# Product 6 of the down parts, and product 5 of the conditioner's, as seven quarter products; scales loaded one number at a time

## The chip, the core and the metric

The kernel runs on one core of a Trainium2 chip. TensorE (PE) multiplies, with its weight loads shown apart as PEld; VectorE (DVE), ScalarE (ACT) and GpSimd (POOL) do the elementwise work; SyncE (SP), ACT and POOL issue the DMAs. The metric is the device time of one execution in microseconds (us). Lower is better. A line number such as L627 is a line of the kernel before.

## The reference

There are 1024 tokens of 512 features in x (8 sequences of 128). Two layers follow each other, each a "conditioner" and a feed-forward part, and each adds its result to x:

```
x = x + L0_ffn(L0_cond(x))
x = x + L1_ffn(L1_cond(x))

L0_cond:  act  = silu(x Wg' + low-rank) * (x Wu' + low-rank)      F = 1376
          down = act Wd' + low-rank(act)                          512 features
L0_ffn:   w_eff = w * (su @ sv)   (for gate, up and down)         I = 1792
          down = (silu(h gate') * (h up')) down'
L1_cond:  x W' + b + 2 * low-rank(x)                              512 x 512
L1_ffn:   W[o, i] = q[o, i] * s[o, i // 128]   (q are small integers)
          down = (silu(h Wg') * (h Wu')) Wd'                      I = 1792
```

The scales of the last part are s_gu, one number for each of 1792 rows, 2 matrices and 4 groups of features, and s_down, one for each of 512 rows and 14 groups. On the chip they are wanted as sg, 128 partitions by 112 numbers, and sd, 128 partitions by 56 numbers.

## The kernel before, in words

Features lie on the partitions (x and h are each four tiles of 128 x 1024) and the tokens along the row, in two halves of 512 (tb = 0 and 1). The stages, by their times in the profile: the conditioner's gate and up (tiles p_c, until 157 us), the conditioner's down part (d_c, 157 to 231), the feed-forward gate and up (p_f, 231 to 397), its down part (d_f, 397 to 481), the last conditioner (l, 481 to 512) and the quantised feed-forward part (gu_q and d_q, to the end).

Both down parts are the one function down() (L601). It is given n blocks of 128 inner features: n = 11 in the conditioner (layer "c", 5 pairs and one left over), n = 14 in the feed-forward part (layer "f", 7 pairs). The output of 512 features by 1024 tokens, seen as a 2 x 2 matrix of blocks, is made by Winograd's seven products in place of eight. Each product has two output tiles m of 128 x 512. The weight forms of the products are a[1] to a[7], and the token forms are called 11, 12, 21, 22 and T1 to T4: T1 = 12 - 11 for product 5, T3 = 22 - 12 for product 7, T2 = 22 - T1 for product 6, T4 = 21 - T2 for product 4. VectorE makes T1 to T4, by one subtraction for each pair (form, L630), and they overwrite dead forms.

A product is carried out in one of two ways. sums() does it whole: a matmul of 128 x 512 for each pair and each m. of_blocks() (L689) applies the same scheme once more inside it: one pair is done plainly, and the other 2 x group pairs (group is 2 in c, 3 in f) as seven quarter products of 128 x 256. In exchange these need token forms of their own (second_tokens, L649: four subtractions on VectorE, 512 columns wide in c, 768 in f), weight forms (second_weights, L661: four operations on POOL), two more PSUM banks z1 and z5, three copies on ACT into a tile r (L718, L722, L725), one addition on VectorE (odd, L627), and the additions of r onto the result. Before the change products 2, 3, 7 and 4 are done of blocks, and 1, 5 and 6 whole. "u" is product 1 plus product 6 and "v" the sum made from product 7; both are added onto several output tiles by VectorE.

The order on each engine is that of the program text (in_order pins it), so an instruction that waits holds up everything behind it on its engine. VectorE's order through the second half of down() is: the tokens of product 3, T3, additions for product 2, tokens of product 7, additions for product 3, T2, T4, tokens of product 4, additions of v, of u, of product 4. In c a hook (three_forms, hook 6) then makes forms T1, T3 and T2 of h for p_f, and T4 is made after the part. In f the last conditioner begins with l_T, the forms of x, T3 first.

There are eight PSUM banks, taken in turn, and r has two buffers. The weight forms s2 also have two. In f, POOL has behind its down work the gathers for the last conditioner's adapters, l_forms (four operations) and the DMAs of the quantised weights wgu_q and wd_q.

The scales are loaded by SP as rows (g_rows 112 x 128 and d_rows, 14 rows), turned by TensorE against an identity matrix, and copied from PSUM to SBUF by VectorE (turn_scales, hook 3, L1298 to L1304), in the middle of the d_f part. The identity is made on POOL.

The ACT engine makes, in each unit of p_c, a Silu that PE's banks wait for; in units f = 2 to 6 it also casts a piece of the feed-forward layer's scales (L453), which SP loads by 12 DMAs a piece (scale_raw, L445). The DMAs of SP and ACT share eight semaphores in turn, and each issue waits for the DMA that was given the same semaphore eight issues earlier.

Of the kernel before, what the change touches and what calls it, by code (L numbers as in the profile page):

```python
# [55 lines left out]
def kernel(  # L56
# [30 lines left out]
    def mm(*args, **kwargs):  # L87
        in_order(nc_mm(*args, **kwargs))  # L88
# [331 lines left out]
    for i, bit in enumerate((2 * RS, RS)):  # L420
# [3 lines left out]
        for low in range(2):  # L424
# [3 lines left out]
            )  # L428

    def scale_piece(pool, i: int):  # L430

# [168 lines left out]

    def down(pool, layer: str, n: int, act, wd0: int, to, plus: bool, dt, hooks, adapters=None):  # L601

# [38 lines left out]


        groups = [slice(i * group, (i + 1) * group) for i in range(2)]
        tokens2 = pool.tile([P, 4, group, quarter], F32, tag="tokens2", name=f"tokens2_{layer}")
        own = [tokens2[:, i] for i in range(4)]
        dead = [b["11"][:, g, bass.ts(q, quarter)] for g in groups for q in range(2)]
        second = {}

        def second_tokens(i: int, src: str, place, in_place: bool):  # L649

            b11, b12, b21, b22 = (
                b[src][:, g, bass.ts(q, quarter)] for g in groups for q in range(2)
            )
            t1, t2, t4, t3 = place
            if in_place:
                t3 = b12
            for t, x1, x2 in ((t1, b12, b11), (t2, b22, t1), (t4, b21, t2), (t3, b22, b12)):
                subtracted(t, x1, x2)
            second["b", i] = {1: b11, 2: b21, 3: b22, 4: t4, 5: t1, 6: t2, 7: t3}

        def second_weights(i: int):  # L661
            a11, a12, a21, a22 = (a[i][:, g, bass.ts(m, P)] for m in range(2) for g in groups)
            s = pool.tile([P, 3, group, P], F32, tag="s2", name=f"s2_{layer}{i}", bufs=2)
            s1, s2, s4 = (s[:, k] for k in range(3))
            weight_forms(nc.gpsimd, a11, a12, a21, a22, s1, s2, s4, True)
            second["a", i] = {1: a11, 2: a12, 3: s4, 4: a22, 5: s1, 6: s2, 7: a21}
# [26 lines left out]
        def of_blocks(i: int, src: str, onto=None, single=None):  # L693
# [4 lines left out]
            for m in range(2):  # L698
                mm(
                    banks[m], a[i][:, pairs - 1, bass.ts(m, P)], b[src][:, pairs - 1],  # L700
                    start=onto is None, stop=True, skip_group_check=onto is not None,
                )
                if single is not None and n % 2:
                    leftover(banks[m], m, *single)
            r = pool.tile([P, 4, quarter], F32, tag="r", name=f"r_{layer}{i}", bufs=2)

# [25 lines left out]

        def onto_output(i: int, src: str, banks, tb: int, more=lambda m: None):
            banks, r = of_blocks(i, src, banks, (0, tb))
            for m in range(2):
                more(m)
                if plus:
                    added(nc.vector, at(m, tb), banks[m], at(m, tb))
                else:
                    in_order(nc.scalar.copy(at(m, tb), banks[m]))  # L740
            for m in range(2):
                added(nc.gpsimd, at(m, tb), at(m, tb), r[m])
# [3 lines left out]
        for j in range(pairs):  # L746
            added(nc.vector, a[5][:, j], wd[1][0][:, j], wd[1][1][:, j])
            form_of(j, "T1", "12", "11")
        second_tokens(2, "21", own, False)
        subtracted(a[6], a[5], a[1])  # L750
        subtracted(a[3], a[2], a[6])
        second_weights(2)
        subtracted(a[7], a[1], a[7])
        banks1, banks5, banks4 = [], [], None
        for m in range(2):
            banks1.append(sums(1, m, "11"))
            in_order(nc.scalar.copy(u[m], banks1[m]))
        hook(1)
        for m in range(2):
            banks5.append(sums(5, m, "T1"))  # L760
        second_tokens(3, "22", dead, False)
        second_weights(3)
        form("T3", "22", "12")
        if adapters is None:
            for m in range(2):
                added(nc.vector, at(m + 2, 1), banks5[m], at(m + 2, 1))
            onto_output(2, "21", banks1, 0)
        else:
            def first_adapters(m: int):
                extra = new(8, m)  # L770
                leftover(extra, m, 1, 1, True)
                adapters(m, [[banks1[m], None], [None, extra]], go_on={(0, 0), (1, 1)})
                in_order(nc.scalar.copy(at(m + 2, 1), extra))
                added(nc.vector, at(m + 2, 1), banks5[m], at(m + 2, 1))

            onto_output(2, "21", banks1, 0, first_adapters)
        second_tokens(7, "T3", own, True)
        second_weights(7)
        if adapters is None:
            onto_output(3, "22", banks5, 1)  # L780
        else:
            banks4 = [new(4, m) for m in range(2)]

            def second_adapters(m: int):
                adapters(
                    m, [[None, banks5[m]], [banks4[m], None]], fresh={(1, 0)}, go_on={(0, 1)},
                )

            onto_output(3, "22", banks5, 1, second_adapters)
        second_weights(4)  # L790
        hook(2)
        form("T2", "22", "T1")
        form("T4", "21", "T2")
        second_tokens(4, "T4", dead, True)
        hook(3)
        banks7, v = of_blocks(7, "T3")
        for m in range(2):
            added(nc.vector, v[m], banks7[m], v[m])
            for tb in range(NTB) if plus else (1,):
                added(nc.vector, at(m + 2, tb), at(m + 2, tb), v[m])  # L800
        for m in range(2):
            added(nc.vector, u[m], sums(6, m, "T2"), u[m])
            for o in (m, m + 2):
                added(nc.vector, at(o, 1), at(o, 1), u[m])
            added(nc.vector, at(m + 2, 0), at(m + 2, 0) if plus else v[m], u[m])
        hook(6)
        banks4, r = of_blocks(4, "T4", banks4, (1, 0))
# [6 lines left out]
    with ExitStack() as c_layer:  # L814
# [116 lines left out]
        for f in range(NF0):  # L931
# [12 lines left out]
            if 3 <= f < 7:  # L944
                down_adapters_a.gather(range(2 * f - 6, 2 * f - 4))
            if f == 8:
                down_adapters_a.arrange(nc.scalar.copy, slice(0, NB))
# [42 lines left out]
        with ExitStack() as top:  # L990

            dt = [x[j // 2][:, bass.ts(j % 2, TB)] for j in range(NF0 // 2)]
            down(
                pool(top, "down_c", "right"), "c", NF0, act_c, NF - NF0, h, False, dt,
                {1: down_low_rank, 6: three_forms}, down_adapters,
            )

# [279 lines left out]

    one = early.tile([P, P], F32, tag="one", name="one")  # L1280
    in_order(nc.gpsimd.memset(one, 1.0))
    for sign in (1, -1):
        in_order(
            nc.gpsimd.affine_select(
                out=one, in_=one, pattern=[[-sign, P]], compare_op=ALU.is_ge,
                fill=0.0, base=0, channel_multiplier=sign,
            )
        )
    g_rows = early.tile([NF * 2 * KC, P], F32, tag="g_rows", name="g_rows")
    nc.sync.dma_start(out=g_rows, in_=s_gu.rearrange("f (c p) -> (f c) p", p=P))  # L1290
    d_rows = early.tile([NF, KC, P], F32, tag="d_rows", name="d_rows")
    nc.sync.dma_start(out=d_rows, in_=s_down.rearrange("f (k p) -> f k p", p=P))
    sg = early.tile([P, NF, 2, KC], F32, tag="sg", name="sg")
    sd = early.tile([P, KC, NF], F32, tag="sd", name="sd")

    def turn_scales():
        ps = bank("scales")
        n = NF * 2 * KC  # L1298
        mm(ps[:, :n], g_rows, one[:n, :n], start=True, stop=True)
        nc.vector.tensor_copy(sg.rearrange("p f s k -> p (f s k)"), ps[:, :n])  # L1300
        ps = bank("scales_down")
        for o in range(KC):
            mm(ps[:, bass.ts(o, NF)], d_rows[:, o, :], one[:NF, :NF], start=True, stop=True)
        nc.vector.tensor_copy(sd.rearrange("p o f -> p (o f)"), ps[:, : KC * NF])  # L1304

    lw = early.tile([P, KC, H], F32, tag="lw", name="lw")
# [16 lines left out]
    with ExitStack() as top:  # L1323
# [3 lines left out]
            down_f, "f", NF, act_all, 0, x, True, [dt[:, j] for j in range(NF // 2)],  # L1327
            {2: for_last_conditioner, 3: turn_scales},
        )
# [157 lines left out]
    def down_group(f: int, o: int, on_act=False):  # L1487
        w, src, scale = ready["q", f][1][:, bass.ts(o, P)], acts["q", f], sd[:, o, f : f + 1]
        both = pair(f"d_q{f}_{o}")
# [118 lines left out]
    def down_out(back: int, o: int, tb: int):  # L1608
        to = x[o][:, halves[tb]]
        f = last_f - back  # L1610
        scaled(to, groups["d", back, o, tb], sd[:, o, f : f + 1], to)
        store(o, tb)

    def down_copied(back: int, o: int, tb: int):
# [6 lines left out]
        f = last_f - back  # L1621
        scaled(ys[back, o, tb], groups["d", back, o, tb], sd[:, o, f : f + 1])

# [111 lines left out]
```

## Time and profile before

| | |
|---|---|
| times of 3 runs | 680.10, 678.46, 680.25 us, median 680.1 |
| the profiled execution | 678.08 us, span 676.4 us |
| granted TensorE clock | 0.997 |
| PE busy | 664.3 us (98%) |
| VectorE busy | 501.2 us (74%) |
| POOL busy | 408.8 us (60%) |
| ACT busy | 193.8 us (29%) |
| d_c, 157 to 231 us | PE 74.0 of 74, VectorE 56.4 |
| d_f, 397 to 481 us | PE 81.7 of 84, VectorE 78.1 |
| l, 481 to 512 us | PE 31.0 of 31, VectorE 19.1 |

The share over the whole span says that TensorE is nearly always busy. The table by stage says more: in d_f VectorE is nearly as full as TensorE. A row of the timeline gives the start, the duration, the engine, the line, the operation, the tiles (out<-in), the shape and how many instructions are drawn together; in brackets stands the idle time ahead of it and what ended that. A matmul of fp32 is recorded as two rows, so "x28" are 14 matmuls. Consecutive VectorE instructions overlap a little, so that a row of 0.67 us costs 0.60 us of the engine.

### The profile page before, as it was taken

The numbers are of one execution on the slowest core, as the hardware profiler recorded it, in microseconds if no ns is written. First come the engines' busy times: TensorE is split into PE (matmuls) and PEld (weight loads), VectorE is DVE, ScalarE is ACT, GpSimd is POOL, SyncE is SP. The second block draws the span as 40 slices with busy tenths as digits, with TensorE's granted clock in tenths as the row PEclk, the third lists the DMA queues.
The fourth block names the chain that finished last, engine by engine and source line by source line (L and its number), as shares of the span: only waits on it lengthen the run. The fifth ranks groups of instructions, "written<-read, shape, count | busy, mean of one in ns | idle before, by whom it ended". The sixth has DMA issues, their size and how long they took to land.

```text
span 676.4 us, 7209 instructions
## 1 busy us (share of the span) xinstructions
PE 664.3 (98%) x2520; PEld 405.1 (60%) x2520; DVE 501.2 (74%) x661; ACT 193.8 (29%) x292; POOL 408.8 (60%) x357
## 2 busy tenths in 40 slices
PE   8999999999999999999999999899999999999995
PEld 3444444444565645665666664685636777788874
DVE  6545435446749887878788679999747888899997
ACT  1212111211021112333323320110115655665563
POOL 5356765441344055667866931597702989898996
PEclk9999999999999999999999999999999999999998
DMA  6501125130002002202200060000851130000003
GB/s 237 197 1 53 63 78 183 63 140 1 0 1 78 31 0 94 93 13 82 94 0 1 0 208 0 1 0 17 292 175 30 41 86 16 16 1 1 1 1 124
DMA packets 18335, 42.48 MB, mean 63 GB/s; under 512 B 3118, under 2 KB 4286, under 8 KB 18172
## 3 DMA queue, kind: packets, MB, share of 16 engines
q1 hardware_dynamic: 11772, 25.71, 11.1%
q0 software_dynamic: 5376, 14.49, 6.9%
q10 hardware_dynamic: 1152, 1.84, 0.8%
q8 instruction: 20, 0.33, 0.2%
q14 instruction: 15, 0.12, 0.0%
HBM read 39.93 MB, written 2.10 MB: 62 GB/s over the span
## 4 chain that ended last, share of the span: by engine, by line
PE 84%; DVE 6%; POOL 6%; issue 2%; DMA 1%; ACT 1%; SPq 0%; POOLq 0%; DVEq 0%; ACTq 0%
PE p_c L88 21%; PE p_f L88 15%; PE gu_q L1450 12%; PE d_c L88 8%; PE d_q L1450 5%; PE d_f L88 4%; PE l L88 4%; PE zb_f L88 3%; PE za_f L88 3%; PE z_f L88 2%; PE z_c L88 2%; DVE act_f L630 1%; POOL sum L1465 1%; PE bank L1450 1%; POOL act_lo L1465 1%
## 5 line engine op out<-in xcount | busy, mean ns | idle before, releaser
L1459 DVE SCALAR_TENSOR_TENSOR sum<-gu_q,sg,sum 128x1024 f32<-128x1024 f32 x65 | 83.0, 1282 | 15.6 <-ACT sum L1456 10.3
L1450 PE MATMUL gu_q<-h_hi,wgu_q 128*128 128x512 f32 x208 | 82.2, 395 | 0.5 <-DVE l_v L1394 0.4
L1450 PE MATMUL gu_q<-h_lo,wgu_q 128*128 128x512 f32 x208 | 81.1, 390 | 0.0
L88 PE MATMUL p_f<-x,s_f 128*128 128x512 f32 x112 | 52.2, 597 | 0.0
L1456 ACT ACTIVATE sum<-gu_q,sg 128x1024 f32<-128x1024 f32 x39 | 43.3, 1113 | 21.9 <-PE gu_q L1450 21.8
L1465 POOL TENSOR_TENSOR sum<-sum,sum 128x1024 f32<-128x1024 f32 (+1 forms) x14 | 32.6, 2328 | 26.8 <-DVE sum L1459 26.8
L1450 PEld LDWEIGHTS gu_q<-h_hi,wgu_q 128*128 128x128 f32 x208 | 39.0, 188 | 13.0 <-DVE x L1459 2.5
L589 DVE TENSOR_TENSOR act_c<-p_c,v_c 128x512 f32<-128x512 f32 x11 | 7.6, 690 | 52.3 <-PE p_c L88 52.3
L1450 PEld LDWEIGHTS gu_q<-h_lo,wgu_q 128*128 128x128 f32 x208 | 39.1, 188 | 7.9
L88 PE MATMUL p_c<-x,raw_c 128*128 128x512 f32 x88 | 43.2, 616 | 0.0
L1465 POOL TENSOR_TENSOR act_lo<-sum,act_hi 128x1024 fp32r<-128x1024 f32 (+1 forms) x15 | 34.0, 2265 | 13.3 <-ACT act_hi L1517 13.3
L1459 DVE SCALAR_TENSOR_TENSOR x<-d_q,sd,x 128x1024 f32<-128x1024 f32 x33 | 42.0, 1275 | 0.0
L88 PE MATMUL p_c<-T_x,raw_c 128*128 128x512 f32 x88 | 41.6, 594 | 0.0
L88 PE MATMUL p_c<-T_x,s_c 128*128 128x512 f32 x88 | 41.2, 592 | 0.0
L88 PE MATMUL p_f<-h,raw_f 128*128 128x512 f32 (+1 forms) x96 | 40.2, 541 | 0.1
L590 POOL TENSOR_TENSOR act_c<-act_c,p_c 128x512 f32<-128x512 f32 x10 | 12.7, 1274 | 42.0 <-DVE act_c L589 33.1
L1465 POOL TENSOR_TENSOR sum<-sum,sil_q 128x1024 f32<-128x1024 f32 (+1 forms) x15 | 34.0, 2265 | 1.7 <-ACT sil_q L1508 1.5
L1450 PE MATMUL d_q<-act_hi,wd_q 128*128 128x512 f32 x88 | 34.8, 396 | 0.0
L1450 PE MATMUL d_q<-act_lo,wd_q 128*128 128x512 f32 x88 | 34.3, 390 | 0.0
L88 PEld LDWEIGHTS p_f<-x,s_f 128*128 128x128 f32 x112 | 20.9, 190 | 19.5 <-issue 16.3
L88 PEld LDWEIGHTS p_c<-T_x,s_c 128*128 128x128 f32 x88 | 16.7, 190 | 21.0 <-issue 19.6
L88 PEld LDWEIGHTS p_c<-T_x,raw_c 128*128 128x128 f32 x88 | 16.6, 190 | 21.3 <-issue 19.7
(345 smaller groups left out, 1498.8 us busy)
## 6 DMA issues: line engine op xcount, KB each, us to landing
raw_f<-in_f_gu_dram SPq DMA_DIRECT2D x14, 512.0 KB
wgu_q<-in_q_gu_dram POOLq DMA_DIRECT2D x14, 512.0 KB, 6.0
raw_c<-in_c_gu_dram SPq DMA_DIRECT2D x10, 512.0 KB
wd<-in_f_down_dram SPq DMA_DIRECT2D x14, 256.0 KB
wd_q<-in_q_down_dram POOLq DMA_DIRECT2D x14, 256.0 KB, 6.1
x<-in_xT_dram SPq DMA_DIRECT2D x11, 256.0 KB
wd<-in_c_down_dram SPq DMA_DIRECT2D x11, 256.0 KB
out_dram<-x SPq DMA_DIRECT2D x6, 256.0 KB
```

The lines of the kernel that those rows point to most:

```text
L88: in_order(nc_mm(*args, **kwargs))
L589: add(act[0], x4, v, ALU.add)
L590: mul(act[0], act[0], p1, ALU.mult)
L630: in_order(nc.vector.tensor_tensor(out_, x1, x2, ALU.subtract))
L1450: nc.tensor.matmul(ps, w, part[:, at], start=(n == 0), stop=(n == len(src) - 1))
L1456: in_order(nc.scalar.activation(to, ps, AF.Identity, scale=scale))
L1459: nc.vector.scalar_tensor_tensor(to, ps, scale, plus, op0=ALU.mult, op1=ALU.add)
L1465: in_order(nc.gpsimd.tensor_tensor(to, a, b, op))
```

## The change

Five things are changed, all but the last in down().

1. Product 6 is done of blocks, in both layers; product 5 too, in c. Each needs second_tokens, second_weights, r, z1 and z5 as above. s2 gets a third buffer. In c, r of product 5 lies in the tile x[3].
2. In f the two additions of product 5's banks onto x, which stood behind product 3's tokens and T3, stand ahead of them.
3. In c two outputs that ACT copied from PSUM (and one that VectorE added) are now made by VectorE additions with r of product 5. The adapters' extra bank is added by VectorE where ACT copied it.
4. The order changes: POOL makes the weight forms of products 3 and 7 earlier; those of 6 and 4 stand ahead of, and behind, POOL's additions of product 3. On VectorE, three token forms of product 6 stand between T2 and T4 and the fourth behind T4; the tokens of product 4 stand behind the additions into v. The additions of u onto the last tile stand behind hook 6.
5. turn_scales, the identity and the row loads are gone. Instead ACT issues two DMAs at unit f = 4 of p_c, behind the cast of a scale piece and ahead of a Silu. They load sg and sd in their final layout, where neighbouring numbers of a row lie 128 numbers apart in DRAM.

```diff
+    sg = const.tile([P, NF, 2, KC], F32, tag="sg", name="sg")
+    sd = const.tile([P, NF, KC], F32, tag="sd", name="sd")
+    def load_scales():
+        in_order(
+            nc.scalar.dma_start(
+                out=sg.rearrange("p f s k -> p (f s k)"), in_=s_gu.rearrange("f (c p) -> p (f c)", p=P)
+            )
+        )
+        in_order(
+            nc.scalar.dma_start(
+                out=sd.rearrange("p f o -> p (f o)"), in_=s_down.rearrange("f (o p) -> p (f o)", p=P)
+            )
+        )
...
+            if f == 4:
+                load_scales()
...
-            s = pool.tile([P, 3, group, P], F32, tag="s2", name=f"s2_{layer}{i}", bufs=2)
+            s = pool.tile([P, 3, group, P], F32, tag="s2", name=f"s2_{layer}{i}", bufs=3)
...
+            if i == 5:
+                r = to_r5.rearrange("p (b t) -> p b t", b=4)
...
+        if adapters is not None:
+            second_tokens(5, "T1", False)
+            second_weights(5)
+        second_weights(3)
...
-        second_tokens(3, "22", dead, False)
-        second_weights(3)
-        form("T3", "22", "12")
         if adapters is None:
+            subtracted(a[7], a[1], a[7])
+            for m in range(2):
+                banks5.append(sums(5, m, "T1"))
             for m in range(2):
                 added(nc.vector, at(m + 2, 1), banks5[m], at(m + 2, 1))
-            onto_output(2, "21", banks1, 0)
+            second_tokens(3, "22", False)
+            form("T3", "22", "12")
+            onto_output(2, "21", banks1, 0, then=lambda: second_weights(7))
         else:
+            second_tokens(2, "21", False)
+            subtracted(a[7], a[1], a[7])
+            banks5, r5 = of_blocks(5, "T1")
+            for m in range(2):
+                added(nc.vector, at(m + 2, 1), banks5[m], r5[m])
+            second_tokens(3, "22", False)
+            form("T3", "22", "12")
...
-                in_order(nc.scalar.copy(at(m + 2, 1), extra))
-                added(nc.vector, at(m + 2, 1), banks5[m], at(m + 2, 1))
+                added(nc.vector, at(m + 2, 1), extra, at(m + 2, 1))
...
-            onto_output(3, "22", banks5, 1, second_adapters)
-        second_weights(4)
+            onto_output(3, "22", banks5, 1, second_adapters, r5, next_weights)
+        if sixth:
+            second_weights(4)
         hook(2)
         form("T2", "22", "T1")
+        if sixth:
+            rest_of_6 = second_tokens(6, "T2", True, True)
         form("T4", "21", "T2")
-        second_tokens(4, "T4", dead, True)
-        hook(3)
+        if sixth:
+            rest_of_6()
         banks7, v = of_blocks(7, "T3")
         for m in range(2):
             added(nc.vector, v[m], banks7[m], v[m])
+        if sixth:
+            second_tokens(4, "T4", True)
+        for m in range(2):
             for tb in range(NTB) if plus else (1,):
                 added(nc.vector, at(m + 2, tb), at(m + 2, tb), v[m])
+        if sixth:
+            banks6, r6 = of_blocks(6, "T2")
         for m in range(2):
-            added(nc.vector, u[m], sums(6, m, "T2"), u[m])
+            if sixth:
+                added(nc.vector, u[m], r6[m], u[m])
+            added(nc.vector, u[m], banks6[m] if sixth else sums(6, m, "T2"), u[m])
             for o in (m, m + 2):
                 added(nc.vector, at(o, 1), at(o, 1), u[m])
+        hook(6)
+        for m in range(2):
             added(nc.vector, at(m + 2, 0), at(m + 2, 0) if plus else v[m], u[m])
-        hook(6)
```

## The prediction

> **What bounds the kernel now.** I read the busy shares first, then the busy times by stage, the waits of TensorE in the stage that changes, and last the timelines of the two down parts.
>
> ```profile
> PE 664.3 (98%) x2520; PEld 405.1 (60%) x2520; DVE 501.2 (74%) x661; ACT 193.8 (29%) x292; POOL 408.8 (60%) x357
> ```
>
> TensorE sets the time, as an average. By stage (start:end, length, then busy time of PE, PEld, DVE, ACT, POOL) the spare time of VectorE is not where the change wants it:
>
> ```profile
> 157.00:231.00 74.00, 74.00 (x313) 42.73 (x310) 56.43 (x75) 11.03 (x22) 22.94 (x20) 1.00 0.06 19
> 397.00:481.00 84.00, 81.68 (x283) 52.69 (x282) 78.08 (x93) 8.60 (x18) 51.18 (x42) 1.00 0.14 47
> ```
>
> In d_f VectorE works 78 of 84 us. TensorE has one wait there, for VectorE:
>
> ```profile
> PE d_f L88 <- DVE x L627: 2.3, 1, 2.3
> ```
>
> TensorE's timeline of d_f from product 3 on shows that wait, the two groups that turn the scales, and product 6 whole (457.89) between product 7 and product 4, which are done of blocks:
>
> ```profile
> 434.83 1.98 PE L88 MATMUL d_f<-act_f,ds_f 128*128 128x512 f32 x4 [2.32 <-DVE x L627]
> ...
> 445.72 0.37 PE L88 MATMUL scales<-one,g_rows 112*128 112x112 f32 x2
> 446.02 1.06 PE L88 MATMUL scales_down<-one,d_rows 14*128 14x14 f32 x8
> 447.01 1.98 PE L88 MATMUL d_f<-act_f,wd 128*128 128x512 f32 x4
> ...
> 457.89 12.18 PE L88 MATMUL d_f<-act_f,ds_f 128*128 128x512 f32 x28
> 469.91 1.88 PE L88 MATMUL d_f<-act_f,wd 128*128 128x512 f32 x4
> ...
> 484.18 3.67 PE L88 MATMUL l<-l_T,lw 128*128 128x512 f32 x8
> ```
>
> VectorE in the same stretch: T2 (seven) beside POOL, T4 (seven) and one token form nearly alone, the scale copies, then the tail up to l_T, which the matmuls of 484.18 read:
>
> ```profile
> 447.04 9.35 DVE L630 TENSOR_TENSOR act_f<-act_f,dt_f 128x512 f32<-128x512 f32 x7
> 456.31 5.34 DVE L630 TENSOR_TENSOR act_f<-act_f 128x512 f32<-128x512 f32 x8
> 461.58 0.26 DVE L1300 COPY sg<-scales 128x112 f32<-128x112 f32 x1
> 461.76 0.94 DVE L630 TENSOR_TENSOR act_f<-act_f 128x768 f32<-128x768 f32 x1
> ...
> 480.21 0.69 DVE L627 TENSOR_TENSOR r_f<-z_f,r_f 128x512 f32<-128x512 f32 x1 [2.67 <-ACT r_f L725]
> ...
> 483.35 1.28 DVE L336 TENSOR_TENSOR l_T<-x,x 128x512 f32<-128x512 f32 x2
> ```
>
> From 447.04 to 484.63 VectorE rests 2.67 us in one wait, and TensorE reaches the product that needs l_T when VectorE is just there. Whoever shortens TensorE's work alone gains nothing past that point.
>
> **The change in f (d_f to l).** TensorE saves the 2.32 us of waiting (the two additions find their banks done at 421.56, when VectorE arrives at 422.40; the tokens behind them come 1.3 later and are still ahead of TensorE's 432.5); the turn, 447.01 - 445.72 = 1.29; and product 6, 12.02 whole against 10.88 (product 7) or 10.78 (product 4) of blocks, 1.2. Sum 4.8: TensorE could begin T3's product of l at 484.18 - 4.8 = 479.4.
>
> VectorE's chain decides. T2 can begin 1.1 earlier, at 446.0: the idle 1.16 us at 445.24 waited for product 3, which is now early. From there to the end of l_T the old chain holds 37.59 - 2.67 = 34.9 of work. Off go the copies, 0.3. On come product 6's odd addition (0.6), r6 onto u (2 x 0.65 = 1.3) and four token forms of 128x768: 0.90 each alone (461.76), 1.70 beside POOL (the row at 437.09), so 3.6 to 6.8; half and half, 5.2. That is 41.7 and l_T ends at 487.7: 3.1 later than before. All of TensorE's 4.8 goes into waits on the way (product 6's banks, r's buffers, which wait for v's last addition, then T3). Low end 486.1, +1.5. High end: POOL makes four more forms of 128x384, 1.0 to 1.6 each, 6.4 at most; VectorE beside POOL runs at half pace (1.34 against 0.67 for one 128x512), so another 3.2, l_T at 492.5, +7.9. I take +3.1, the middle of the token rows without the collisions: part of what POOL gains in work it takes from stretches in which it meets VectorE already. What stands behind: T2's product of l needs two more pairs, 3.5 after T3 before and after. POOL's l_forms ended at 475.8; 6.4 later is still ahead of 487.68.
>
> **A rule against the row.** VectorE's 128x512 subtraction costs 1.34 us beside POOL and 0.67 nearly alone in the two rows above. The Trainium skill, "SBUF — State Buffer", section "Who interferes with whom", calls it an exclusive lock: a VectorE instruction with two SBUF inputs and a GpSimd one that reads SBUF take turns, the loser blocked for the whole instruction. By it the four forms of product 6 would stop VectorE for their whole length, 6.4 where my high end has 3.2, and l_T would end some 3 us later than that end. The halved pace of the row decides for me.
>
> **The change in c (d_c to p_f).** TensorE saves at product 6 8.59 (212.52 to 221.11) against 7.86 of blocks, and at product 5 8.69 against 7.86: together 1.6. VectorE worked without a gap from T2 at 203.21 to 228.57, when T2 of h was done, waited 1.97, and ended T4 of h at 234.95; p_f wanted those at 232.30 and 237.98. On the chain come two additions at product 3 that ACT did as copies (1.2), four token forms of 128x512 (2.4 alone to 4.8 beside POOL), the odd addition 0.6 and r6 onto u 1.3: 5.5 to 7.9. It starts 0.85 earlier. Two additions of u (1.2) go behind T2 of h. T2 of h: 228.57 - 0.85 - 1.2 + 5.5 to 7.9 = 232.0 to 234.4, against TensorE's new 230.7. T4: 234.95 - 0.85 - 1.97 + 5.5 to 7.9 = 237.6 to 240.0 against 237.98 before. So p_f comes 0.3 earlier to 2.1 later; I take +1. Product 5's tokens and forms (earlier, off this chain) have the time of its plain pair, 1.7, and of product 1 to be ready: cover 162 to 172 us; gone, each us of delay would eat the 0.83 saved.
>
> **The scales (ACT's queue, 76.6 us).** 128 x 112 + 128 x 56 = 21,504 numbers, none next to another in DRAM: 1,344 packets for each of 16 DMA engines. Packets of 4 bytes took 7 to 9 ns (median 9) each in this trace, but no DMA here had more than 128 of them. By that 9.4 to 12.1 us, done at 86 to 91 with the landing. Who waits: SP's scale_raw issues of the next piece (from 83.7, the semaphores come round at 85.7), and behind those ACT's cast, with a Silu queued behind it:
>
> ```profile
> 77.00 0.60 ACT L588 ACTIVATE p_c<-p_c 128x512 f32<-128x512 f32 x1 [0.44 <-PE p_c L88]
> ...
> 89.53 0.62 ACT L453 CAST scale_parts<-scale_raw 128x512 fp32r<-128x512 f32 x1 [10.00 <-DMA scale_raw<-in_f_si_dram]
> 90.30 0.60 ACT L588 ACTIVATE p_c<-p_c 128x512 f32<-128x512 f32 x1
> ```
>
> TensorE writes the bank that a Silu frees some 3 us later (77.60 to 80.46), so this costs 0 to 2.3; I take 0.6. If a packet costs what one of 512 bytes did (27 ns), 36 us, done at 113: about +24, the high end. The issue itself took 0.25 to 0.45 us for 14 as for 128 runs, no slope; held for the 12 us that the packets take, it would cost 12 - 3 = 9. SP's two loads and POOL's identity go at no gain: neither was waited for.
>
> The Trainium skill speaks against this part: "DMA: Bandwidth & Descriptors", "Rules for kernel authors", says that a strided last dimension becomes one descriptor per element and is to be rearranged. Its table under "Measured" gives some 10.5 ns a packet, an estimate of 14 us in place of my 12; 2 us more than the row, no other sign.
>
> **The sum**: 678.1 (the profiled execution, span 676.4 and 1.7 around it) + 3.1 + 1 + 0.6 = 682.8, say 683. That execution lies 2.0 under the median of the three runs, 680.1.
>
> **Rivals.** (A) the forecast, 679 to 688: VectorE takes over both down parts. Chance 0.46.
>
> (B) VectorE's additions are hidden and TensorE's savings come through. Place: T2 at 446. Point: l_T must end before 483 (1.6 earlier than before, to outweigh c and the scales). Price: T2's seven alone instead of beside POOL give back 9.35 - 4.67 = 4.7 (f at 3.1 - 4.7 = -1.6), and the four tokens at 0.90 another 1.6; with c at -0.3, 678.1 - 3.2 - 0.3 = 674.6; were everything hidden, 678.1 - 4.8 - 1.6 = 671.7. For it: forms of product 7 now leave POOL earlier. Against: POOL gets four forms more, put right where T2 runs. Chance 0.23.
>
> (C) The element loads hold ACT or the semaphores: 682 + 9 to 24, 691 to 706. For it: no such load in this trace. Against: the short packets measured. Chance 0.21.
>
> (D) Savings and additions cancel, or the moved additions only trade the wait for the next, 676 to 680. Chance 0.10.
>
> **Numbers from these.** A measurement tells 0.3%, 2.0 us, from no change. Faster: B, 0.23. Same: D and the edge of A and B, 0.11. Slower: A and C, 0.66. The range leaves out B's far end and C's far half: 674.5 to 698; A alone is 679 to 688.
>
> **What would show it.** Right: in d_f no wait at product 3, no scales groups, but TensorE waits for VectorE at product 6, at z1 of product 4 or at the l_T matmuls, some 5 us or more in sum, and VectorE without a gap from 446 on; in c a wait at z5 of product 6 or at p_f's second product. Wrong: TensorE goes from product 6 to l without waits (B), ACT's Silu behind 77 is late or scale_raw lands late (C), or VectorE's T2 rows shorten to 0.67. My weakest term is how much of VectorE's work meets POOL's.

## The result: 12.6 us slower, and the profile after

The changed kernel takes 691.89 us in the median (4 runs, 691.26 to 692.29) against 679.31 before: a ratio of 1.0182, interval 1.0167 to 1.0197. Its profiled execution took 689.7 us from first to last instruction, 13.3 more than before.

TensorE's share fell to 97% although its busy time barely moved (1.6 us more, with half-speed stretches in it); its list of waits, which had one long entry in the stages changed, now has five. The columns are: waiting engine, tile and line, what it waited for, total, times, longest.

```profile
PE 665.9 (97%) x2552; PEld 414.0 (60%) x2552; DVE 519.6 (75%) x682; ACT 194.8 (28%) x297; POOL 418.9 (61%) x366
```

```profile
PE z_c L88 <- DVE r_c L645: 3.3, 1, 3.3
PE z_f L88 <- ACT r_f L751: 3.2, 1, 3.2
PE d_f L88 <- DVE act_f L648: 2.7, 1, 2.7
PE p_c L88 <- ACT p_c L567: 1.9, 1, 1.9
PE l L88 <- DVE l_T L336: 1.8, 1, 1.8
```

The first is product 6 of c, the second product 4 of f, the third product 6 of f, the fourth lies in p_c and the fifth in l. To see where the time came from I take the start of TensorE's first matmul of each stage, in both traces and in those of all experiments, and compare stage lengths (us):

| kernel | start to d_c | d_c to p_f | p_f to d_f | d_f to l | l to end |
|---|---|---|---|---|---|
| before | 157.1 | 73.5 | 167.0 | 83.2 | 195.7 |
| after | 162.3 | 76.9 | 167.0 | 85.8 | 197.7 |
| e1_scales | 162.0 | 73.5 | 167.0 | 83.5 | 195.9 |
| e2_moved | 157.0 | 73.5 | 167.0 | 80.6 | 195.7 |
| e3_turned | 157.9 | 77.1 | 167.0 | 89.2 | 195.1 |
| e4_whole6 | 161.8 | 72.7 | 167.0 | 79.2 | 195.8 |
| e5_late_loads | 161.6 | 72.7 | 167.0 | 79.2 | 195.9 |
| e6_fill | 157.8 | 73.5 | 167.0 | 83.2 | 195.8 |
| e7_order | 161.5 | 74.0 | 167.6 | 85.8 | 197.5 |
| e8_r4 | 161.6 | 75.4 | 166.9 | 82.5 | 203.7 |
| e9_idle_loads | 157.7 | 72.7 | 167.0 | 79.2 | 195.9 |
| e10_turn1 | 157.8 | 72.7 | 166.9 | 80.1 | 195.6 |
| e11_swap | 157.4 | 72.6 | 167.0 | 79.2 | 195.8 |
| e12_no_tokens6 | 161.4 | 78.3 | 167.0 | 82.6 | 195.8 |

Where nothing in p_c was changed, the first stage varies from 157.0 to 157.9 from trace to trace (TensorE's waits for the first loads of x, at 7 to 9 us in e9, are part of that). The rest is steadier, so the 13.3 us are 5.2 in p_c, 3.4 in d_c, and 4.7 from d_f on.

**p_c, 5.2.** ACT's timeline of the changed kernel, its DMA issues included: sg goes out in 0.39 us, and the issue of sd holds the engine for 9.49, with the Silu and the copy of p_c behind it.

```profile
76.62 0.39 ACTq L436 DMA_DIRECT2D sg<-in_s_gu_dram  x1
77.03 9.49 ACTq L441 DMA_DIRECT2D sd<-in_s_down_dram  x1
86.63 0.60 ACT L604 ACTIVATE p_c<-p_c 128x512 f32<-128x512 f32 x1 [9.41 <-issue]
...
87.64 0.58 ACT L567 COPY p_c<-p_c 128x512 f32<-128x512 f32 x1
98.23 0.62 ACT L469 CAST scale_parts<-scale_raw 128x512 fp32r<-128x512 f32 x1 [10.01 <-DMA scale_raw<-in_f_si_dram]
```

The next cast is late as well, at 98.23 (89.53 before): POOL, which frees the buffer of scale_raw, waited 8.74 us for the held Silu, and SP issued the next piece only from 92.45 on (83.69 before).

TensorE waits for the copy at 87.64, and then something else is to be seen: two groups of four rows take 2.60 and 3.06 us where such a group takes 1.88.

```profile
84.52 1.88 PE L88 MATMUL p_c<-T_x,raw_c 128*128 128x512 f32 x4
88.27 2.60 PE L88 MATMUL p_c<-x,raw_c 128*128 128x512 f32 x4 [1.87 <-ACT p_c L567]
90.68 3.06 PE L88 MATMUL p_c<-x,s_c 128*128 128x512 f32 x4
```

The busy times by stretch (start:end, length, PE busy, granted clock, DMA share, GB/s) name it: TensorE's clock is granted at half for some 3 us after the wait.

```profile
86.00:88.00 2.00, 0.40 (x1) 1.00 0.88 6
88.00:89.00 1.00, 0.73 (x2) 1.00 0.83 6
89.00:90.00 1.00, 1.00 (x3) 0.75 0.81 6
90.00:91.00 1.00, 1.00 (x3) 0.50 0.89 6
91.00:92.00 1.00, 1.00 (x2) 0.50 0.88 6
92.00:93.00 1.00, 1.00 (x2) 0.54 0.00 0
93.00:94.00 1.00, 1.00 (x8) 1.00 0.06 16
```

In this trace the wait costs 2.0 and the slow stretch 1.9 (88.27 to 93.67 is 5.40, the same matmuls took 3.52 before); 0.6 is another short wait at 105.7 and 0.6 the start. That the half clock sets the price does not follow: e4, below, shows the same length without it.

**d_c, 3.4.** Product 6's quarter with z5 waits 3.3 us for the odd addition of product 7, which stands behind T2, T4 and the tokens of 6 on VectorE, and the next group is slow again:

```profile
218.59 1.03 PE L88 MATMUL z_c<-act_c,ds_c 128*128 128x256 f32 x4
222.93 2.05 PE L88 MATMUL z_c<-tokens_c,s_c 128*128 128x256 f32 x4 [3.32 <-DVE r_c L645]
224.77 1.66 PE L88 MATMUL d_c<-act_c,ds_c 128*128 128x256 f32 x4
```

VectorE's rows show what stands ahead of that addition (222.11): T2, three tokens of product 6, T4 and the fourth token.

```profile
209.73 6.26 DVE L648 TENSOR_TENSOR act_c<-act_c,x 128x512 f32<-128x512 f32 x5
...
218.49 3.69 DVE L648 TENSOR_TENSOR act_c<-act_c 128x512 f32<-128x512 f32 x6
222.11 0.68 DVE L645 TENSOR_TENSOR r_c<-z_c,r_c 128x512 f32<-128x512 f32 x1
```

The gap is 3.5 (219.45 to 222.93), the half clock 1.6, and the two products of blocks give back 1.6.

**d_f and l, 4.7.** VectorE's timeline of the changed kernel has no rest from 430 to 501. Three of its rows are longer than those that answer to them before: product 3's tokens with T3 (11.77 before), T2 (9.35), and four additions of v onto x (2.8 before), which now fall beside POOL's l_forms. Six additions of u onto x are shorter in return, 3.6 against 6.4: before the change it was they that met l_forms.

```profile
431.21 13.94 DVE L648 TENSOR_TENSOR act_f<-act_f 128x768 f32<-128x768 f32 x11
...
455.59 9.63 DVE L648 TENSOR_TENSOR act_f<-act_f,dt_f 128x512 f32<-128x512 f32 x7
465.15 8.14 DVE L648 TENSOR_TENSOR act_f<-act_f 128x768 f32<-128x768 f32 x11
...
479.33 6.77 DVE L645 TENSOR_TENSOR x<-x,r_f 128x512 f32<-128x512 f32 x4
...
496.52 1.28 DVE L336 TENSOR_TENSOR l_T<-x,x 128x512 f32<-128x512 f32 x2
```

Counted from the first matmul of d_f, l_T ends at 91.7 (497.80 - 406.14) against 87.1 before: 4.6 later.

### The profile page after: what moved, and what is told of

It reads as the page before. It is cut to its first block, busy times and chain, and to the rows that moved or that the text cites. A ratio compares the mean times of both kernels' runs of the same rounds, so it can differ in the third digit from the quotient of the medians.

```text
span 689.7 us, 7314 instructions
## 1 busy us (share of the span) xinstructions
PE 665.9 (97%) x2552; PEld 414.0 (60%) x2552; DVE 519.6 (75%) x682; ACT 194.8 (28%) x297; POOL 418.9 (61%) x366
## 4 chain that ended last, share of the span: by engine, by line
PE 66%; DVE 15%; POOL 8%; issue 5%; DMA 2%; SPq 1%; ACT 1%; ACTq 0%; DVEq 0%; POOLq 0%
PE p_f L88 15%; PE p_c L88 13%; PE gu_q L1491 12%; PE d_c L88 6%; PE d_q L1491 5%; DVE act_f L648 5%; PE l L88 4%; PE zb_f L88 3%; PE za_f L88 3%; PE z_c L88 3%; DVE x L645 2%; DVE tokens_f L648 1%; SPq L461 1%; POOL sum L1506 1%; DVE act_c L648 1%
## 5 line engine op out<-in xcount | busy, mean ns | idle before, releaser
L1506 POOL TENSOR_TENSOR act_lo<-sum,act_hi 128x1024 fp32r<-128x1024 f32 (+1 forms) x15 | 33.9, 2262 | 13.3 <-ACT act_hi L1558 13.3
L88 PEld LDWEIGHTS p_c<-x,raw_c 128*128 128x128 f32 x88 | 16.3, 196 | 23.0 <-issue 18.8
```

The lines of the kernel that those rows point to most:

```text
L1506: in_order(nc.gpsimd.tensor_tensor(to, a, b, op))
```

## The experiments

The theory after the two traces: three separate prices, each in its own stage. The element loads hold ACT in front of something TensorE needs; in c product 6 makes TensorE wait because of the order on VectorE; in f VectorE has become the bound. The half clock stands beside each; where it adds, the experiments must tell.

**Each part alone, or taken back.** e1 is the kernel before with load_scales in place of turn_scales:

```diff
+            if f == 4:
+                load_scales()
...
-            {2: for_last_conditioner, 3: turn_scales},
+            {2: for_last_conditioner},
```

> The kernel before with only the scales part of the change (two element loads by ACT at f = 4, no turning). Theory, that the parts add up stage by stage as the two traces stand: sd's issue holds ACT for 9.5 us, TensorE waits 2 us for the Silu'd bank and then runs some 3.5 us at half clock, p_c ends 4.5 to 5.1 us later; the turn's 1.3 us in d_f comes off: 679.3 + 3.2 to 3.8 = 682.5 to 683.1. Rival, that the loads cost what the prediction took (0 to 2.3): 678.6 to 680.3. Rival, that the late p_c was an accident of another part of the change: 678.0.

681.57 us against 679.59, ratio 1.0034 (1.0021 to 1.0046). p_c is 4.9 longer, as in the changed kernel, so the price is the loads' own. The total is under the 682.5 I expected because my base, the median of the kernel before, was too high: it holds a stretch of half clock in most runs (e6), and four of e1's six runs, at 681.4 to 681.6, do not; they lie 3.4 above the quick runs of before near 678.1. The profiled execution, 683.55, is the slowest of the six: in it the old wait at product 3 of d_f (2.32) is followed by half clock, which takes back the turn's 1.3.

e2 is the kernel before with the two additions moved:

```diff
+        if adapters is None:
+            for m in range(2):
+                added(nc.vector, at(m + 2, 1), banks5[m], at(m + 2, 1))
         second_tokens(3, "22", dead, False)
         second_weights(3)
         form("T3", "22", "12")
         if adapters is None:
-            for m in range(2):
-                added(nc.vector, at(m + 2, 1), banks5[m], at(m + 2, 1))
             onto_output(2, "21", banks1, 0)
```

> The kernel before with only the two additions of f moved ahead of product 3's tokens. Theory: the wait of 2.3 us at product 3 goes and nothing takes its place, since VectorE's tail rests 2.67 us for product 4: 679.3 - 2.3 = 677.0. Rival, VectorE is the bound all through d_f and the wait comes back at product 7 or at l: 678.2 to 679.3.

675.51 against 679.59, ratio 0.9941 (0.9925 to 0.9958): 4.1 faster where I expected 2.3. The stage shortened by 2.6. The rest is in the base: the profiled execution of before (678.08) is one of its quicker runs. Runs of e2 lie within 0.4 us of each other, those of before fall into two groups, near 678.2 and near 679.9.

e3 is the changed kernel with rows loaded and turned as before (sd by one matmul in place of four):

```diff
+    d_rows = early.tile([NF * KC, P], F32, tag="d_rows", name="d_rows")
+    nc.sync.dma_start(out=d_rows, in_=s_down.rearrange("f (k p) -> (f k) p", p=P))
...
+        n = NF * KC
+        mm(ps[:, :n], d_rows, one[:n, :n], start=True, stop=True)
+        nc.vector.tensor_copy(sd.rearrange("p f o -> p (f o)"), ps[:, :n])
...
+        hook(3)
         banks7, v = of_blocks(7, "T3")
```

> The changed kernel without the element loads: rows are loaded by SP and turned on TensorE as before, sd by one matmul in place of four (0.5 us on TensorE in all, two copies on VectorE, 0.3). Theory: p_c is as before, 4.5 to 5.1 us less; the turn's 0.5 is lost in the later waits for VectorE, whose copies add 0.3: 691.9 - 4.2 to 4.8 = 687.1 to 687.7. Rival, the price in p_c is not the loads': 692.4.

687.84: 4.05 less than after, 0.1 above what was expected; p_c is as in the kernel before. d_f to the end is 0.7 longer (284.3 against 283.6), as much as the turn takes of TensorE (447.52 to 448.18), so it is not shown that the waits swallow the turn. The clock differs here: it is full behind product 6's wait in f, and the wait at product 4 is 4.86 in place of 3.24. So the 1.6 that half clock costs in the changed kernel behind product 6 is no loss there; at full clock TensorE only waits longer for VectorE.

e4 makes product 6 whole again and keeps all else:

```diff
-        sixth = True
+        sixth = False
```

> The changed kernel with product 6 whole again in both layers; product 5 of c stays of blocks, the moved additions and the element loads stay. Theory, that product 6 is what VectorE can't carry: the waits at product 6, at z1 of product 4 and at l_T go, and the half clock behind them; in c 0.8 is left of the saving, in f 2.3 + 1.3; with 4.5 to 5.1 for the loads 679.3 - 4.4 + 4.8 = 679.7 (678.5 to 681). Rival, the reordering and the additions with r5 cost as much as product 6: 684 to 688.

678.15 against 679.59, ratio 0.9979 (0.9969 to 0.9989), a little under the 678.5 to 681 expected, with p_c still 4.7 too long. No wait is left in d_c or d_f. c is 0.8 shorter than before (product 5 of blocks is worth what the rows said), d_f 4.0 shorter. So of the change only product 6 and the loads are bad; the rest gains.

In p_c the clock stays full here, and the time is the same: behind the wait for the copy (1.85) TensorE waits twice more, the second time for an addition that stands on VectorE behind the work on the late cast (97.76).

```profile
90.23 1.95 PE L88 MATMUL p_c<-x,s_c 128*128 128x512 f32 x4 [0.43 <-DVE act_c L582]
...
105.24 1.95 PE L88 MATMUL p_c<-x,s_c 128*128 128x512 f32 x4 [1.48 <-DVE act_c L582]
```

From the group ahead of the hold to the one that stands two units later (`p_c<-t_gu`, 75.84 and 102.42 before) TensorE takes 26.6 us before, 31.1 and 31.3 with half clock (after, e1) and 30.6 to 31.2 with full clock (e4, e7, e8, e12). So the price in p_c is the hold and the cast that it delays, and the half clock only fills time that would be waited.

**Which mechanism: the loads.** e5 issues them behind the unit's finishing operations, e9 behind product 1 of d_f, e11 there in the other order; all with product 6 whole.

```diff
-            if f == 4:
-                load_scales()
...
             if f:
                 finishing()
...
+            if f == 4:
+                load_scales()
```

> Product 6 whole, as in e4, with the two element loads issued a little later: behind the unit's Silu and copies, where ACT rests 10 us. Theory, that only the held issue in front of a Silu costs: the Silu is on time, d_c begins at 157 as in the kernel before, 678.15 - 4.7 = 673.4 (672.8 to 674.2). Rival, that the 21,504 packets or the shared semaphores hold up SP's scale_raw loads, issued from 83.7 on beside them: the cast of 89.5 is late and 675.5 to 678.

678.01: the theory's time was missed, and the rival's delay was there too. The copy of p_c still stood behind the loads and came 8.13 late, and TensorE waited 2.00 for it, as in the changed kernel:

```profile
79.32 8.29 ACTq L441 DMA_DIRECT2D sd<-in_s_down_dram  x1
87.65 0.59 ACT L567 COPY p_c<-p_c 128x512 f32<-128x512 f32 x1 [8.13 <-issue]
97.45 0.62 ACT L469 CAST scale_parts<-scale_raw 128x512 fp32r<-128x512 f32 x1 [9.21 <-DMA scale_raw<-in_f_si_dram]
```

The cast is late too (97.45, before 89.53), now by the semaphores: two of SP's scale_raw issues waited until 89.83 and 94.12 for those that sg and sd had, so both loads together needed 15.2 us to land. TensorE has no wait for that cast in this trace, as half clock behind the first wait had delayed it already; what the late cast alone would cost was not run.

```diff
-            if f == 4:
-                load_scales()
...
-            {2: for_last_conditioner},
+            {1: load_scales, 2: for_last_conditioner},
```

> Product 6 whole (as e4), with the two element loads issued by ACT behind product 1 of d_f, where it rests 14 us and nothing waits for it. Theory, that the price of the loads in p_c is the held issue before something TensorE needs and the late landing before the scale_raw loads, both of which lie elsewhere here: p_c ends at 157 as before, c keeps -0.8, d_f -4.0: 678.15 - 4.7 = 673.4 (672.5 to 674.2). Rival, the 21,504 packets themselves disturb whatever runs beside them: over 675.

673.46 against 679.52, ratio 0.9911 (0.9894 to 0.9928). ACT is held 8.38 us as ever, and rests 14.44 there:

```profile
409.90 8.38 ACTq L441 DMA_DIRECT2D sd<-in_s_down_dram  x1
424.49 0.37 ACT L751 COPY r_f<-z_f 128x256 f32<-128x256 f32 x1 [14.44 <-PE z_f L88]
```

p_c is as short as before (26.6 us between the two groups named under e4). This version beats both kernels.

> Product 6 whole, with the scales turned on TensorE as in the kernel before, sd by one matmul in place of four. Theory: as e9, and 0.5 to 0.6 of TensorE's time more: 673.9 (673 to 674.8). Rival, that turning costs nothing because something else waits: equal to e9 within 0.3.

e10 is e4's down part with the turn of e3. 674.31, 0.85 more than e9 (0.5 to 0.6 expected): the loads in a place where nobody waits save what the turn costs.

> As e9 with the two element loads in the other order, sd (7,168 numbers) first. If an issue is held until the packets of the one before it have drained, sg, now second, is held for about half of the 8.3 to 9.5 us that sd was, some 4 to 5 us or less, and sd goes out in 0.4. If sd's own shape is slow to issue, sd is held again and sg goes out in 0.4. The time is that of e9 in both cases.

The first issue is again 0.39 and the second, now sg, 4.36 long; the time 673.73 (one run). So it is not the shape: an issue is held for as long as the size of the load ahead of it asks. 14,336 numbers are 896 for each of 16 engines in 8.38 us, 9.4 ns each; 7,168 in 4.36 us, 9.7 ns. The hold ends a little before the last packet of that load starts (418.28 and 419.17 in e9, 413.96 and 414.95 in e11), so whether the engine waits for the packets themselves, or for something that is done ahead of each of them, is not shown.

```profile
409.17 0.39 ACTq L436 DMA_DIRECT2D sd<-in_s_down_dram  x1
409.60 4.36 ACTq L441 DMA_DIRECT2D sg<-in_s_gu_dram  x1
```

**Which mechanism: the clock.** e6 is the kernel before with two idle matmuls in front of product 3 of d_f:

```diff
+            if i == 3 and plus:
+                for j in range(2):
+                    mm(z1, a[5][:, j, bass.ts(0, P)], chunk("T1", j), start=True, stop=True)
             for m in range(2):
```

> The kernel before with two matmuls of 128x512 put in ahead of product 3 of d_f, written to a bank that product 3 then overwrites: 1.7 us more work for TensorE, in the 2.3 us in which it waits. Theory, that the runs of before near 679.9 are those in which the wait at product 3 is followed by half clock and those near 678.1 the ones without: the wait shrinks to 0.6, the clock stays, every run at 677.9 to 678.3, so 1.4 faster than the median of before by adding work. Rival, that the two groups of times have another cause: median 679.3 to 679.8 and the same spread.

678.47 against 680.02, ratio 0.9980 (0.9971 to 0.9989), 0.2 above what the theory gave: more work, less time. All 11 runs lie from 678.0 to 678.9, while the 17 of before beside them had 4 near 678.5 and 13 from 679.6 to 680.35. Its trace has a wait of 0.62 and full clock. So the two groups of before go with this wait; no run of its slow group was profiled. The same wait of 2.32 stands in the traces of before and of e1; in the one the clock is full behind it, in the other half (stretches of before, then of e1):

```profile
432.00:434.80 2.80, 0.51 (x3) 1.00 0.00 0
434.80:436.00 1.20, 1.17 (x3) 1.00 0.00 0
436.00:437.00 1.00, 1.00 (x4) 1.00 0.06 16
```

```profile
439.70:441.00 1.30, 1.25 (x3) 0.98 0.00 0
441.00:442.00 1.00, 1.00 (x2) 0.50 0.00 0
442.00:443.00 1.00, 1.00 (x3) 0.50 0.00 0
443.00:444.00 1.00, 1.00 (x4) 0.50 0.00 0
```

**Which mechanism: product 6.** e7 lets VectorE make T4 and the last token of 6 behind product 7's additions:

```diff
-        form("T4", "21", "T2")
...
         banks7, v = of_blocks(7, "T3")
         for m in range(2):
             added(nc.vector, v[m], banks7[m], v[m])
-        if sixth:
-            second_tokens(4, "T4", True)
+        form("T4", "21", "T2")
+        rest_of_6()
+        second_tokens(4, "T4", True)
```

> The changed kernel with T4 and the last token of product 6 moved behind product 7's additions into v, in both layers (VectorE does the same work in another order). Theory for c, that the wait at z5 of product 6 is order: the odd addition of product 7 comes some 3.5 earlier, the wait of 3.3 shrinks under 2 and may move to the seventh quarter product, c gains 2 to 4. Theory for f, that VectorE's sum is the bound: d_f to gu_q stays within 1 of 119.8. Together 688 to 690. Rival, that the order is to blame in f too: d_f to gu_q under 117, 684 to 686.

688.78, 3.1 less than after, as the theory had it for both layers. In c the wait of 3.3 becomes one of 1.27 and one of 0.41, with full clock, and the stage loses 2.9 (the 1.6 of half clock in it); p_f takes 0.6 more. In f the way from the first matmul of d_f to that of gu_q is 118.8 against 119.8. Even so c is 1.3 longer than with product 6 whole.

e8 gives product 4's r in f a place of its own:

```diff
-            if i == 5:
+            if i == (4 if plus else 5):
                 r = to_r5.rearrange("p (b t) -> p b t", b=4)
...
-            {2: for_last_conditioner},
+            {2: for_last_conditioner}, None, None, dt[:, :2].rearrange("p a t -> p (a t)"),
```

> The changed kernel with r of product 4 in f put into the dead tokens T1, so that ACT's copy into it no longer waits for product 7's r to be free. Theory, that VectorE, busy from 430 to 501 without a rest, sets the end: the wait of 3.2 at z of product 4 goes and comes back at l_T, 691.2 to 692.2. Rival, that the buffers set it: 688.3 to 689.5.

693.56, slower by 1.7 and above both expectations. The wait for r is gone and d_f 3.3 shorter, but all of it is back at l_T: 5.1 in place of 1.8, and half clock behind it, which no expectation had. (The trace is that of the quickest of four runs, 692.25.)

```profile
PE l L88 <- DVE l_T L336: 5.1, 1, 5.1
```

e12 leaves out the four token subtractions of product 6 in f, so that this product is made from old data:

```diff
+            left_out = i == 6 and plus
             for t, x1, x2 in ((t1, b12, b11), (t2, b22, t1), (t4, b21, t2)):
-                subtracted(t, x1, x2)
+                if not left_out:
+                    subtracted(t, x1, x2)
...
-                subtracted(t3, b22, b12)
+                if not left_out:
+                    subtracted(t3, b22, b12)
```

> The changed kernel with the four token subtractions of product 6 left out in f (so product 6 of f is made from old data); all else as in the changed kernel. They take some 3.9 us of VectorE there (eleven operations in 8.14 us, of which T4's seven at 0.61 are 4.3). Theory, VectorE's chain from T2 to l_T sets the end of d_f: d_f to gu_q falls by those 3.9, from 119.8 to about 115.9, and the time to 687.4 to 688.6. Rival, TensorE's own waits (for the last T2 at product 6, the half clock behind it, r at product 4) set it: d_f to gu_q falls by less than 1.5, 690.4 or more.

686.39, 5.5 less than after and 1.0 under the expected range. From d_f to gu_q it is 114.6, 5.2 less than after, where the subtractions were 3.9: VectorE's chain is the bound, and what moved forward also met less of POOL (the four additions of v take 2.49 in place of 6.77, those of u more). The waits at product 4 and at l_T are gone.

## Why the prediction was wrong

The sign was right and the time lies in the range; the forecast of 683 is 9 short. In the profiled executions the sum said 4.7 where 13.3 came. By its terms:

- **The scales, 0.6 taken, 4.5 measured.** The step that failed is "The issue itself took 0.25 to 0.45 us for 14 as for 128 runs, no slope". That was true of the issue and said nothing of the next one: sd was held for 9.5 us. The hold stood in the rival as 12 - 3 = 9, and the 3 was a wrong reading: the matmuls that the text has wait for the Silu at 80.46 were on time in the changed kernel (81.09), although the Silu came at 86.63. What TensorE came for was the copy behind it, which ended at 79.5 before, and it came at 85.6; so its slack was some 6 and the first wait 2.0. The rest is the late cast, which the text names and takes at 0 to 2.3, with the semaphores as its reason; in the changed kernel it was POOL's buffer. The loads were done at 92, where the text had 86 to 91; 9.4 to 9.7 ns a number lie between the row's 9 and the 10.5 that the text took from "Measured". The rule weighed there, "Rules for kernel authors" in "DMA: Bandwidth & Descriptors" of the Trainium skill, had the right side.
- **c, 1 taken (-0.3 to 2.1), 3.4 measured.** The savings were right (0.8 for product 5 in e4). The cost was looked for where p_f reads T2 of h. It came earlier, at z5 of product 6, which the text names among the signs but prices nowhere: product 7's odd addition stands behind all of T4 and the tokens. e7 shows that 2.9 of it are this order and the half clock behind its wait.
- **f, 3.1 taken (1.5 to 7.9), 4.6 measured at l_T.** The mechanism was right, and e8 and e12 show it: no wait taken from TensorE gains anything while VectorE ends where it ends. The term that was wrong is the start of T2: it was to come 1.1 earlier and came no earlier (49.5 us behind the first matmul of d_f in both), since POOL's forms of product 7, now ahead, fell beside product 3's tokens and T3 (13.94 against 11.77). Such collisions stand in the high end at 3.2 and in the sum at nothing. From T2 to the end of l_T the chain holds 42.2 where the text had 41.7, by luck so close: the four tokens of product 6 took 3.9 and not 5.2, T2, the tokens of product 4 and the additions onto x 1.9 more than before.
- **The half clock, in no term.** Its 1.6 in c add to the time (75.4 us with full clock in e8, 76.9 here). In p_c its 1.9 would have been waited for the late cast (e4), and in f its 1.6 behind product 6's wait for VectorE (e3). The price of the wait at product 3, 2.3 in the text, was 4.1 against the median of before (e2), and the 2.0 between its profiled execution and its median go with that, too.

The misses, 3.9 for the scales, 2.4 and 1.5, and the 0.6 by which the two traces differ at the start, make 8.4, with 4.7 13.1 of the 13.3.

The signs of (A) came in c and f, and those of (C) in p_c: the Silu and scale_raw were late. That 691.9 lies at the near end of (C)'s 691 to 706 is chance, since the loads cost half of its lowest price and c and f more than its base.

The lock rule cannot be judged here: l_T came 4.6 later, inside the bounds from the halved pace and far from the 11 that the text's sum by the rule adds up to, but no run sets the two apart.

## What to carry to other kernels

When an engine off the critical path is full in one stage, count its work there and not over the span: a saving on TensorE in that stage only turns into waits, and a saved buffer wait moves to the next reader. Before an element-wise DMA is put into a queue, look for a place where that engine rests for as long as all packets take, since the next issue and everything behind it is held; the same loads cost 4.7 us in one place (e4) and nothing that shows in another (e9). Price a wait of TensorE of 2 us or more with the slow stretch that can follow it, and then ask whether TensorE would only have waited in that time for something else.

## What the runs showed of the hardware

A wait of TensorE can be followed by half the clock, and whether it is does not depend on the wait alone. The wait of 3.32 at z5 of product 6 stands in four traces of the same instructions with d_c lengths of 75.4 (e8, full clock), 76.9 (after), 77.1 (e3) and 78.3 us (e12, half clock for some 6 us). Stretches of e8, then of e12:

```profile
222.00:223.50 1.50, 1.21 (x6) 1.00 0.00 0
223.50:225.00 1.50, 1.50 (x9) 1.00 0.04 11
```

```profile
222.00:223.50 1.50, 1.47 (x4) 0.50 0.04 11
223.50:225.00 1.50, 1.50 (x5) 0.50 0.00 0
225.00:226.50 1.50, 1.50 (x5) 0.50 0.00 0
226.50:228.00 1.50, 1.50 (x5) 0.51 0.00 0
228.00:230.00 2.00, 2.00 (x10) 1.00 0.00 0
```

In the changed kernel the wait of 3.24 at product 4 of f had none, the shorter one of 1.87 in p_c had one.

The clock records of the traces say what these cases have in common. In all fourteen, the stretches between two changes of the granted clock last whole multiples of 3.413 us: 3.41 or 6.83 at half clock, and 81.92 (24 of them), 129.71 (38) and 238.93 (70) at full clock in the changed kernel. So the clock is set on a beat of 3.41 us, and the beat lies differently in each trace (its first change to full clock comes at 4.5 to 7.6 us). Cut into these beats, TensorE's idle time sorts the cases: behind a beat at full clock with 2.0 us of idle or more half clock followed all eleven times, with 1.82 or less never, and in between it went both ways (1.87 half, 1.94, 1.97 and 1.97 full). The wait of 3.32 has 3.01, 3.25 and 2.44 us in one beat in after, e3 and e12, and is split into 1.78 and 1.55 in e8. The wait of 2.32 at product 3 is split into 1.20 and 1.12 in the trace of before and has 2.21 in one beat in e1. The wait of 3.24 is split into 1.97 and 1.27.

The Trainium skill, "TensorE: Matmul & The Clock Gate", Part 1, tells of an activity window of some 3.4 us that runs free of the program and of half rate after an idle one. The beat agrees with that window; that 2.0 us of idle in 3.41 are enough does not agree with a whole idle window. No run was made to test this reading, and what decides between 1.82 and 2.0 stays open.
